# The first group's route in the fifth batch, and its rows stored in slot order as 16-bit halves and loaded turned

## The chip, the cores and the metric

One core of a Trainium2 chip. The time is the device time of one execution in microseconds (us), measured around the program; the profile's span is the part of it in which instructions are recorded. Engines: PE (TensorE) multiplies and turns, DVE (VectorE) and ACT (ScalarE) do elementwise work and read PSUM, POOL (GpSimd) does elementwise work and issues all indirect DMAs (gathers and scatters), SP (SyncE) issues the plain and the transposing DMAs. Each engine runs its instructions in program order and waits on semaphores.

## What is computed

The input x is (8, 512, 128) in fp32: 8 batches of 512 tokens of 128 features. The reference, cut to what matters (fp32; `LN` is a layer norm without gain):

```python
x = x + 0.5 * ffn(LN(x))             # fp4 quantized and dequantized in blocks of 16, inner size 352
x = x + attention(LN(x))             # 16 heads of 64, softmax over 512 keys, output projection
x = x + 0.5 * ffn(LN(x))             # the same weights again
x = x + 0.5 * moe(LN(x))             # 8 experts, the best 2 for each token, inner size 256
x = x + linear_attention(LN(x))      # 6 layers with residual, gain and bias
x = x + 0.5 * moe(LN(x))             # the same experts again
```

In `moe`, each token is gated with `x @ Wg.T`, its two best experts are taken with softmaxed weights, and each expert computes `(h1 * sigmoid(h1) * h2) @ W3.T` with `h1 = x @ W1.T`, `h2 = x @ W2.T`.

## The kernel before, in words

**Tiles.** One batch is a tile of 128 partitions x 4 chunks x 128 features. x of all 8 batches stays in SBUF (`xs`). Everything is fp32; 16-bit types serve only to move fp32 data through the transposing DMA, as two halves of each number.

**Start.** `load_x` loads the batches. The weights of the fp4 FFN are loaded into a pool of their own (`wraw`, L300 to L308), quantized (`quantize`, L425 to L470: scale on DVE, product on POOL, rounding on DVE), turned on PE (L492, L498), and that pool is closed. Then the FFN of batch 0 runs (`feed_forward`, L510): x is quantized (L446 to L467), turned (L419), multiplied by gate and up (L535), `h` is quantized in two halves, turned (L576) and multiplied by the down weights (L594); L619 adds to x.

**Attention.** `attention` (L630) goes through 64 pairs of heads, g = 0 to 63, eight a batch, about 16.8 us each. `scores` and `softmax` (L684 to L718) give `pe`; POOL copies it into halves (`pe_h`, L712), SP stores it (`pe_d`), and SP's transposing DMA brings part of it back turned (`aT`); the rest is turned on PE (L741). `widen` (L771 to L779) makes on POOL the tile `wide` from the row sums, which SP stores (`wide_d`) and loads turned as `r`; DVE needs it for `oT` (L763). `times_v` (L755) multiplies with the values, and after eight pairs `project_out` (L796) adds to x (L800). The list `ORDER` (L806) is written by hand: for each pair it says in which order PE and SP get `scores`, `transfer`, `turn`, `times_v`, `project` of this pair, the pair before and the next one. DVE, ACT and POOL follow a scheduler there.

Four slots of `ORDER` are called "ffn". In each, `beside()` (L861) takes one step of a queue of other work: the first FFN of a later batch (queued at "next", two pairs before the batch two ahead), the second FFN of a finished batch (queued when `project_out` has run), and `first_route` (L1605), the route of group 0 (batches 0 to 3), queued after the second FFN of batch 5, at g = 48. A step ends ahead of each PE operation; `Plan.pause` makes an empty step. `Route` (L954) normalizes the four tiles (`xh`), stores them in DRAM (`xg`, L970), gates them on PE (L980), picks the two best experts (`choose`, L1000), ranks the tokens in each expert by a PE product (`ranks`, L1013), gives each a place in 40 slots of 128 rows (`bases`, `places`), and from these makes the tables `tokens` (which token stands in a row; `tokens_part`, L1096: DVE and POOL make `in_slot` and `at_row` at L1103 to L1118, PE sums at L1126), `places` and `rows`. After that, `first_route` gathers the first two quads (4 slots each) of rows.

**After attention.** From here all five engines follow `Plan.order` (L115), which lists operations by planned costs in ns, with critical paths as priorities and an offset per stage from the table `LATER` (L62), which makes a stage's operations less urgent by so many ns (more urgent if negative). The stages: the second FFN of batch 7; experts of group 0 (phase 0); route and experts of group 1 (batches 4 to 7), called (0,1); the linear attention of 6 layers for two batches at a time (`linear`, L1401); then route and experts of both groups again (phase 1).

`experts` (L1213) takes 10 quads of 4 slots. For each: 4 gathers on POOL bring the rows of 4 slots (`xgs`, L1193), PE turns them (`turn4`, L419), ACT copies the turned tile (`xgT`, L1233), PE multiplies (L1245), ACT and DVE form `g` (L1250, L1254), PE turns it (L1273) and ACT copies it (`gT`, L1278), PE multiplies by W3 (L1293), ACT copies `yo` (L1302). The results go to DRAM, either scattered to the tokens' places by 4 scatters on POOL (`yt`, L1309; groups with phase equal to group) or stored in slot order by SP (`yg`). `combine` (L1338) then loads (L1347, after scatters) or gathers (L1362, after stores) two results for each token and DVE adds them (L1370). Tiles of a quad are taken from rings of 2 (xgs: two early ones and one); the next user waits for the last user of the tile.

The linear layers' weights (about 2 MB) are loaded by SP at the start of this part.

Of the kernel before, what the change touches and what calls it, by code (L numbers as in the profile page):

```python
# [17 lines left out]
P = 128  # L18
# [26 lines left out]
class Op:  # L45
# [16 lines left out]
    ("combine", 0, 1): 7000,  # L62
    ("combine", 1, 0): -31000,
    ("combine", 1, 1): 152000,
    ("experts", 0, 0): 6000,
    ("experts", 1, 0): 91000,
    ("experts", 1, 1): 33000,
    ("linear", 0): 11000,
    ("linear", 2): 7000,
    ("linear", 6): 5000,  # L70
    ("route", 1, 0): -8000,
    ("route", 1, 1): 76000,
# [3 lines left out]
class Plan:  # L76
# [38 lines left out]
    def order(self, banks):  # L115
        ops = [x for x in self.ops if x is not None]
        rank = {}
        for op in ops[::-1]:
            op.next = []
        for op in ops:  # L120
            for x in op.after:
                x.next.append(op)
        for op in ops[::-1]:
            rank[op] = op.ns + max((rank[x] for x in op.next), default=0)
        waits = {op: len(op.after) for op in ops}
        left = {op: len(op.users) for op in ops}
        ready = {e: [] for e in ("PE", "DVE", "ACT", "POOL", "SP")}
        free = dict.fromkeys(ready, 0)
        events, number, done = [], 0, []
        bank_of = {}  # L130

        def at(t, what, x):
            nonlocal number
            number += 1
            heapq.heappush(events, (t, number, what, x))

        for op in ops:
            if not waits[op]:
                at(0, "ready", op)
        banks = list(banks)  # L140
        while events:
            now = events[0][0]
            while events and events[0][0] <= now:
                _, _, what, x = heapq.heappop(events)
                number += 1
                if what == "ready":
                    heapq.heappush(ready[x.engine], (x.behind - rank[x], number, x))
                elif what == "bank":
                    banks.append(x)
            for e, heap in ready.items():  # L150
                if free[e] > now:
                    continue
                kept = []
                while heap:
                    item = heapq.heappop(heap)
                    op = item[-1]
                    if op.bank and not banks:
                        kept.append(item)
                        continue
                    if op.bank:  # L160
                        bank_of[op] = banks.pop(0)
                    done.append(op)
                    busy = max(op.ns - self.STARTS.get(e, 0), 20)
                    if e == "POOL" and op.ns > 3000:
                        busy = 1250
                    if e == "SP":
                        busy = 360
                    free[e] = now + busy
                    at(free[e], "free", None)
                    end = now + op.ns  # L170
                    for x in op.next:
                        waits[x] -= 1
                        x.start = max(getattr(x, "start", 0), end + self.SEMAPHORE)
                        if not waits[x]:
                            at(x.start, "ready", x)
                    for x in op.after:
                        if op in x.users:
                            left[x] -= 1
                            if not left[x]:
                                at(end, "bank", bank_of[x])  # L180
                    break
                for item in kept:
                    heapq.heappush(heap, item)
        assert len(done) == len(ops)
        return [(op, bank_of.get(op)) for op in done]
# [25 lines left out]
STORE = 3600  # L211


@with_exitstack
def macaron_kernel(
# [83 lines left out]
    of_weights = ExitStack()  # L299
    wpool = of_weights.enter_context(tc.tile_pool(name="wq4", bufs=1))  # L300
    wraw = wpool.tile([P, NW], F32, name="wraw")
    nc.vector.memset(wraw[:, 2 * P : 3 * P], 0.0)
    nc.vector.memset(wraw[:, 5 * P : 6 * P], 0.0)
    for i, w in enumerate((w_gate, w_up)):
        for r, (k0, kn) in enumerate(FK):
            col = (3 * i + r) * P
            nc.scalar.dma_start(wraw[:kn, col : col + P], w[k0 : k0 + kn, :])
    nc.scalar.dma_start(wraw[:, 6 * P :], w_down)  # L308
# [171 lines left out]
    with of_weights, misc_pool("w_m", 2) as misc:  # L480
        plan = Plan()
        wq4, _ = quantize(
            plan, lambda name, shape: wpool.tile(shape, F32, name=name), lambda: wraw, "w4", NW, []
# [26 lines left out]
    def feed_forward(plan, t, mem, after=None):  # L510
# [89 lines left out]
        for c in range(NC):  # L600
            for i in range(2):
                hidden(c, i)
                if c == 3 and i == 0:
                    parts.append(turn([0, 1], [0, 1], qs))
            if c % 2 == 1:
# [4 lines left out]
                qs.append(op)  # L610
        for _ in range(WAIT):
            plan.pause()
# [17 lines left out]
    def attention(first_route):  # L630
        scale = DH**-0.5
        with tc.tile_pool(name="a_sb", bufs=2) as sb, tc.tile_pool(
# [159 lines left out]
            def project_out(b):  # L792
# [19 lines left out]
                ("turn_old", 3),  # L812
                ("scores", 1),
                ("project", 1),
                ("project", 2),
                ("transfer", 0),
                ("ffn",),
# [5 lines left out]
                ("next",),  # L823
                ("ffn",),
# [12 lines left out]
            def ffn(t):  # L837
                plan = Plan()
                feed_forward(plan, t, mem)
# [7 lines left out]
            for _ in ffn(0):  # L847
# [20 lines left out]
            for g in range(NPT + 1):  # L868
                new, old, nxt = g < NPT, g > 0, g + 1 < NPT
                for what, *args in ORDER:  # L870
                    if what == "ffn":
                        beside()
                    elif what == "scores" and new:
# [22 lines left out]
                    elif what == "out" and old and g % NPAIR == 0:  # L896
                        b = g // NPAIR - 1
                        project_out(b)
                        if b < NB - 1:
                            queue.append([ffn(b), 0, -1])  # L900
                        if b == NB - 3:
                            queue.append([first_route(sb), 0, -1])
                    elif what == "next":
                        if g % NPAIR == NPAIR - 2 and g // NPAIR + 2 < NB:
# [3 lines left out]
            while queue:  # L908
                beside()
            pe_order.close()  # L910
# [20 lines left out]
            dram.tile([MG * TT, D], F32, name=f"xg{i}"),  # L931
            dram.tile([NR * P if i else 2 * MG * TT + NR * P, D], F32, name=f"yg{i}"),
# [21 lines left out]
    class Route:  # L954


        def __init__(self, plan, tiles, after, xg, mem, place, name):
# [6 lines left out]
            def tile_part(i):  # L964
# [3 lines left out]

                def store(_):
                    nc.sync.dma_start(  # L970
# [20 lines left out]
                stores.append(plan.add("SP", STORE, store, [a]))  # L991
# [92 lines left out]
            ch = plan.add("DVE", 12 * 290 + 600, choose, taken)  # L1084
            rk = plan.add("PE", product(n * E, 2), ranks, [ch], bank=True)
# [58 lines left out]

            for k in range(2 * MG):
# [51 lines left out]

    class Ring:
# [14 lines left out]
    def experts(plan, route, tiles, xg, yt, rings, spacer, number, last, scattered, early, stage):  # L1213
# [4 lines left out]
        def quad(q):  # L1218
            ks = range(q * QS, (q + 1) * QS)
            (x, x_after), (xT, xT_after) = xgs.take(), xTs.take()  # L1220
# [8 lines left out]
                for s in range(min(QS, NS - q * QS) if q >= early else 0)  # L1229
            ]  # L1230
            t = plan.add("PE", turns(QS), lambda ps: turn4(ps, x), [*got, *xT_after], bank=True)
            turned = plan.add(
                "ACT", act(TT), lambda _: nc.scalar.copy(flat(xT), t.tile), uses=[t]  # L1233
            )
            xgs.used(t)
# [365 lines left out]
    EARLY = 2  # L1601
    kept = {}
    early_xgs = [const.tile([P, QS, D], F32, name=f"xgs{q}") for q in range(EARLY)]

    def first_route(sb):  # L1605
# [9 lines left out]
        def place(what, i):  # L1615
            if what == "xh":
                return norm.tile([P, NC, D], F32, name="xh", tag="xh")
            return sb.tile([P, TT], F32, name="xqT", tag="xqT")

        plan = Plan()  # L1620
        r = Route(plan, xs[:MG], [None] * MG, scratch[0][0], mem, place, "r0")
        yield from plan.steps(banks["misc"], "misc")
        r.over()
        kept["route"] = r
        for q in range(EARLY):
            for s in range(QS):
                gather(early_xgs[q], q, s, r, scratch[0][0])
# [4 lines left out]
    with tc.tile_pool(name="post", bufs=1) as post, tc.tile_pool(  # L1632
# [3 lines left out]
        def new(name, shape, dtype=F32):  # L1636
            return post.tile(shape, dtype, name=name, tag=name)

        wqkv_sb = load(
            "wqkv_sb", [P, DEPTH, 2 * D], w_qkv[:, :, : 2 * D].rearrange("l d c -> d l c"), nc.sync, post  # L1640
        )
        wvT_sb = load("wvT_sb", [P, DEPTH, D], w_vT.rearrange("l d c -> d l c"), nc.sync, post)
        wout_sb = load("wout_sb", [P, DEPTH, D], w_out.rearrange("l d c -> d l c"), nc.sync, post)
        bout_sb = load("bout_sb", [P, DEPTH, D], b_out.partition_broadcast(P), nc.sync, post)
        weights = (wqkv_sb, wvT_sb, wout_sb, bout_sb)
        ys = [new(f"y{b}", [P, NC, D]) for b in range(NB)]
# [3 lines left out]
        def rings(name):  # L1650
            return [
                Ring(
                    (early_xgs if what == "xgs" else [])
                    + [new(f"{what}{name}{i}", shape) for i in range(n)]
                )
                for what, n, shape in (
                    ("xgs", 1, [P, QS, D]),
# [56 lines left out]
        for ph in range(2):  # L1714
            for g in range(2):
                bs = range(g * MG, (g + 1) * MG)
                tiles = [xs[b] for b in bs]
                xg, *yts = scratch[g]
# [7 lines left out]
                if ph:  # L1726
# [5 lines left out]
                    finals(g) if ph else None, g == ph, 0 if g or ph else EARLY, (ph, g),  # L1732
                )
# [18 lines left out]
        for op, bank in plan.order(range(8)):  # L1752
# [51 lines left out]
```

## Time and profile before

| | before |
|---|---|
| time, median of 3 runs | 1904.55 us (1903.48 to 1907.25) |
| the profiled execution's own time | 1905.12 us |
| its span | 1903.4 us |
| its mean PE clock | 0.943 |
| start, up to the first FFN's end for batch 0 | 0 to 58 us |
| attention, up to the last `project_out` | about 66 to 1146 us |
| experts of group 0 and 1, phase 0, PE's part | 1148 to 1346 us |
| linear attention, first PE operation after its wait | from 1394 us |
| experts, phase 1, to the end | to 1903 us |

In the profile's lines an instruction group is shown as line, engine, operation, output <- inputs, with shapes and count. "[4.11 <-DVE rsum L775]" says that the engine was idle for 4.11 us before it, and what it waited for last. In a list of waits the columns are: the waiting operation, what released it, total us, times, longest. DMA-issuing instructions of SP do not count as busy time; those of POOL (DMA_INDIRECT) appear in the timeline with the time they hold POOL.

### The profile page before, as it was taken

The page shows a single profiled execution, that of the slowest core. Times are in us where ns is not written, and L with a number is a line of the kernel's source. Part 1 is how long each engine was busy: PE and PEld are TensorE (multiplying, and loading weights), DVE is VectorE, ACT ScalarE, POOL GpSimd, SP SyncE. Part 2 cuts the span into 40 slices and gives each one's busy share as a digit, 9 for nine tenths or more (in the row PEclk, how much of TensorE's full clock was granted, in tenths as well). Part 3 has the DMA queues.
Part 4 walks back from the last instruction along what each step waited for, and adds up shares of the span by engine and source line. Part 5 has one row for each costly group of instructions (what it writes and reads, how often), then busy time and mean ns, then how long its engine had stood idle before and what let it go on. Part 6 is the DMA issues. An engine that isn't in the chain of part 4 may idle for free.

```text
span 1903.4 us, 32313 instructions
## 1 busy us (share of the span) xinstructions
PE 1679.7 (88%) x10249; PEld 1137.9 (60%) x10249; DVE 1284.4 (67%) x3266; ACT 1072.2 (56%) x2842; POOL 955.7 (50%) x1643
## 2 busy tenths in 40 slices
PE   2799999999999999999998998989659998798953
PEld 2455655656556556556665566656548887666632
DVE  4465766776776776676667657557879998666543
ACT  2466666566675675666763554445447776353521
POOL 1334454353453453443443537676664444375775
PEclk9799999999999999999998999799979999698977
DMA  5377667568666675775774772125100000022323
GB/s 167 80 171 168 144 153 183 140 151 185 154 147 149 167 172 141 166 176 134 171 183 101 177 172 78 55 46 125 44 15 1 1 1 1 23 64 61 75 75 101
DMA packets 439253, 215.10 MB, mean 113 GB/s; under 512 B 349648, under 2 KB 392848, under 8 KB 439088
## 3 DMA queue, kind: packets, MB, share of 16 engines
q1 hardware_dynamic: 428608, 192.95, 42.7%
q0 software_dynamic: 9536, 19.55, 4.5%
q8 instruction: 86, 1.41, 0.3%
q14 instruction: 79, 0.65, 0.1%
q10 hardware_dynamic: 944, 0.54, 0.1%
HBM read 28.53 MB, written 100.53 MB: 68 GB/s over the span
## 4 chain that ended last, share of the span: by engine, by line
PE 48%; DVE 24%; POOL 10%; ACT 9%; issue 5%; DMA 3%; SPq 0%; POOLq 0%; DVEq 0%; ACTq 0%
PE pS L691 8%; PE po L755 8%; ACT pe L703 4%; PE pT L741 3%; PE bank L1245 3%; DVE nmax L700 3%; PE bank L1293 2%; PE bank L535 2%; PE bank L594 2%; PE pv L677 2%; PE bank L1126 2%; PE pk L669 2%; PE bank L419 2%; POOL yt L1309 2%; PE pq L663 2%
## 5 line engine op out<-in xcount | busy, mean ns | idle before, releaser
L703 ACT ACTIVATE pe<-pS,nmax 128x512 f32<-128x512 f32 x512 | 348.4, 688 | 168.1 <-DVE nmax L700 137.0
L700 DVE TENSOR_REDUCE nmax<-pS 128x2 f32<-128x1024 f32 x256 | 310.6, 1214 | 75.0 <-PE pS L691 74.5
L712 POOL COPY pe_h<-pe 128x1024 uint16<-128x1024 uint16 x256 | 272.7, 1092 | 153.0 <-ACT pe L703 74.2
L691 PE MATMUL pS<-kT,qT 64*128 64x512 f32 x1024 | 291.9, 647 | 0.2
L755 PE MATMUL po<-aT,v 128*64 128x256 f32 x2048 | 237.6, 383 | 3.0 <-DMA aT<-pe_d 2.1
L779 POOL COPY wide<-rsum 128x512 uint16<-128x512 uint16 x128 | 76.5, 627 | 290.7 <-DVE rsum L775 290.7
L755 PEld LDWEIGHTS po<-aT,v 128*64 128x64 f32 x2048 | 142.2, 137 | 118.3 <-ACT pe L703 23.5
L1245 PE MATMUL bank<-wall,xgT 128*128 x320 | 150.9, 609 | 6.7 <-ACT xgT L1233 4.9
L741 PE MATMUL pT<-ident,pe 128*128 128x128 f32 x1024 | 137.3, 276 | 4.8 <-ACT pe L703 4.6
L741 PEld LDWEIGHTS pT<-ident,pe 128*128 128x128 f32 x1024 | 116.9, 141 | 23.0 <-ACT pe L703 17.8
L744 ACT COPY aT<-pT 128x512 f32<-128x512 f32 x192 | 107.5, 599 | 22.6 <-PE pT L741 21.0
L1254 DVE SCALAR_TENSOR_TENSOR g<-g,bank 128x256 f32<-128x256 f32 x160 | 66.7, 417 | 74.5 <-ACT g L1250 74.2
L691 PEld LDWEIGHTS pS<-kT,qT 64*128 64x128 f32 x1024 | 77.7, 186 | 57.7 <-issue 44.9
L556 DVE SCALAR_TENSOR_TENSOR h<-h,bank 128x176 f32<-128x176 f32 x120 | 39.5, 329 | 105.1 <-ACT h L553 105.1
L535 PEld LDWEIGHTS bank<-wgu,xqT 128*128 128x128 f32 x480 | 77.4, 197 | 47.0 <-issue 18.9
L419 PE MATMUL bank<-ident,work 128*128 128x128 f32 x436 | 72.4, 293 | 35.9 <-DVE work L402 25.1
L703 ACT ACTIVATION_READ_ACCUMULATOR pe<-pS,nmax 128x1 f32 x512 | 103.6, 202 | 0.0
L535 PE MATMUL bank<-wgu,xqT 128*128 128x176 f32 x480 | 97.5, 329 | 6.3 <-ACT xqT L531 4.3
L1250 ACT ACTIVATE g<-bank 128x256 f32<-128x256 f32 x160 | 60.0, 386 | 67.0 <-PE bank L1245 52.9
L1245 PEld LDWEIGHTS bank<-wall,xgT 128*128 128x128 f32 x320 | 56.7, 193 | 66.1 <-issue 31.7
L763 DVE TENSOR_TENSOR oT<-po,r 128x256 f32<-128x256 f32 x128 | 51.9, 419 | 65.5 <-DMA r<-wide_d 43.2
L1498 ACT ACTIVATE work<-bank,nmk 128x128 f32<-128x128 f32 x192 | 68.1, 370 | 45.8 <-DVE nmk L1490 44.8
(400 smaller groups left out, 3675.4 us busy)
## 6 DMA issues: line engine op xcount, KB each, us to landing
pe_d<-pe_h SPq DMA_DIRECT2D x256, 256.0 KB, 2.4
wide_d<-wide SPq DMA_DIRECT2D x64, 256.0 KB, 2.0
aT<-pe_d SPq DMA_TRANSPOSE x256, 3.9
xg<-work SPq DMA_DIRECT2D x12, 256.0 KB, 2.6
yg<-yo SPq DMA_DIRECT2D x10, 256.0 KB, 3.3
yt<-yo SPq DMA_DIRECT2D x10, 256.0 KB, 2.3
x<-in_x SPq DMA_DIRECT2D x8, 256.0 KB, 4.6
yk<-yg SPq DMA_DIRECT2D x8, 256.0 KB, 4.2
```

Of the source, the lines that this page charges most:

```text
L419: nc.tensor.transpose(ps[:, c, :], src[:, c, :], ident)
L535: nc.tensor.matmul(ps[:, j * FH : (j + 1) * FH], m["xqT"][:, c * P : (c + 1) * P], wgu[:, j, cols], start=True, stop=True,)
L691: nc.tensor.matmul(ps[:, j, :], qTs[g][rows, c * P : (c + 1) * P], kTs[g][rows, :], start=True, stop=True,)
L700: nc.vector.tensor_reduce(nmax, ps, AX.X, ALU.max, negate=True)
L703: nc.scalar.activation(pe[:, j, :], ps[:, j, :], AF.Exp, bias=nmax[:, j : j + 1], accum_out=sums[g][:, 2 * c + j : 2 * c + j + 1],)
L712: nc.gpsimd.tensor_copy(split, pe[:, j, :].bitcast(U16).rearrange("p (n h) -> p h n", h=2))
L741: nc.tensor.transpose(ps[:, k, :], pe[:, j, k * P : (k + 1) * P], ident)
L744: nc.scalar.copy(dst, ps)
L755: nc.tensor.matmul(po[rows, :], vs[g][:, k, rows], aT[:, :, j, k, :], start=(k == 0), stop=(k == NC - 1),)
L779: nc.gpsimd.tensor_copy(split[:, h, :].rearrange("p (n d) -> p n d", d=DH), src[:, h, :, None].to_broadcast([P, NC * 2, DH]),)
L1245: nc.tensor.matmul(ps, xT[:, s, :], wall[:, bass.ds(at[s], 2 * HID)], start=True, stop=True)
L1498: nc.scalar.activation(c4(ek)[:, c, :], pk.tile[:, c * D : (c + 1) * D], AF.Exp, bias=nmk[:, i, c : c + 1], accum_out=sk[:, i, c : c + 1],)
```

## The change

1. **Start.** The fp4 weights are loaded into the memory of the attention's `oT` tile, within `attention`. The FFN of batch 0 takes its first three steps, then the weights are quantized, then it goes on. For this one FFN (`alone`) the first turns of `h` come after all 16 gate and up products instead of before the last pair.
2. **The queue.** The first FFN of batch 7 is queued at g = 40 and `first_route` right behind it, when batch 4's output is projected (before: g = 46 and g = 48). In `Route`, three pauses come after `choose` and two before the token parts.
3. **Halves.** For group 0 in phase 0 POOL copies `xh` into 16-bit halves (`divide`, four copies of 128x1024, in the ring of `pe_h`) and SP stores these.
4. **Sorting.** Once the route is done, each pair has three "sort" slots: in each POOL gathers one slot's 128 rows of halves (64 KB, ring of 6 tiles), and SP stores the slot gathered before in slot order. After 40 slots quad 0 is loaded turned. What is not done by the last pair is done behind it.
5. **Experts of group 0, phase 0.** SP loads each quad turned by one transposing DMA (128x1024 of 16 bits, `xgT`); the gathers, PE's turns and ACT's copies of these ten quads are gone. The ring of `xgs` gets two tiles of its own.
6. **Linear weights.** They are loaded when 80 operations of the plan are out, instead of at the beginning.
7. **`LATER`.** Offsets change: combine(1,0) from -31000 to 109200, route(0,1) new at -105500, route(0,0) new at 28300, experts(1,1) 33000 to 53300, combine(1,1) 152000 to 138200, the others by less than 1000.

In the program order that follows, the experts of phase 1 look so on POOL: before, one scatter, 32 gathers of combine(1,0), 38 scatters; after, the scatters with runs of 1, 2, 4 and 2 combine gathers between them, and the last 24 gathers behind them. The final stores of batches 4 to 7 come ahead of those of 0 to 3.

```diff
 LATER = {
-    ("combine", 1, 0): -31000,
-    ("combine", 1, 1): 152000,
-    ("experts", 1, 1): 33000,
+    ("combine", 1, 0): 109200,
+    ("combine", 1, 1): 138200,
+    ("experts", 1, 1): 53300,
+    ("route", 0, 0): 28300,
+    ("route", 0, 1): -105500,
...
-                if c == 3 and i == 0:
+                if c == 3 and i == 0 and not alone:
                     parts.append(turn([0, 1], [0, 1], qs))
...
+        if alone:
+            parts.append(turn([0, 1], [0, 1], qs[:1]))
...
                 ("turn_old", 3),
+                ("sort",),
                 ("scores", 1),
                 ("project", 1),
                 ("project", 2),
                 ("transfer", 0),
+                ("sort",),
                 ("ffn",),
...
                 ("next",),
+                ("sort",),
                 ("ffn",),
...
-            for _ in ffn(0):
+            wraw = weights_mem("wraw", [P, NW])
+            load_weights(wraw)
+            first = ffn(0)
+            for _ in range(3):
+                next(first)
+            quantize_weights(wraw, weights_mem, misc)
+            for _ in first:
                 pass
...
+                        if b == NB - 4:
+                            queue.append([ffn(NB - 1), 0, NB - 1])
+                            queue.append([first_route(sb), 0, -1])
                         if b < NB - 1:
                             queue.append([ffn(b), 0, -1])
-                        if b == NB - 3:
-                            queue.append([first_route(sb), 0, -1])
...
+                def divide(_):
+                    r["xh_h", i] = place("xh_h", i)
+                    nc.gpsimd.tensor_copy(
+                        r["xh_h", i].rearrange("p (c h d) -> p c h d", h=2, d=D),
+                        r["xh", i].bitcast(U16).rearrange("p c (d h) -> p c h d", h=2),
+                    )
...
             ch = plan.add("DVE", 12 * 290 + 600, choose, taken)
+            for _ in range(3):
+                plan.pause()
...
+            for _ in range(2):
+                plan.pause()
             for k in range(2 * MG):
                 tokens_part(k)
...
+    def load_turned(xT, there):
+        nc.sync.dma_start(
+            flat(xT).bitcast(U16), there.rearrange("s p h d -> (s p h) d"), transpose=True
+        )
...
+                if q >= early:
+                    turned = plan.add(
+                        "SP", LOAD_TURNED, lambda _: load_turned(xT, in_order[q]), [*xT_after]
+                    )
...
+    def sorting(sb):
+        r = kept["route"]
...
+        for k in range(NR):
+            x = sb.tile([P, 2 * D], U16, name="rows", tag="rows", bufs=6)
+            nc.gpsimd.indirect_dma_start(
+                x, None, scratch[0][1][:, :],
+                bass.IndirectOffsetOnAxis(ap=r.tokens[:, k : k + 1], axis=0),
+            )
+            if stores:
+                nc.sync.dma_start(*stores.pop())
+            stores.append((there[k // QS][k % QS].rearrange("p h d -> p (h d)"), x))
+            yield 1
...
+            if i == 80:
+                load_linear()
```

## The prediction

> **What bounds the kernel now.** I read the shares of the page first, then the windows by stage, then PE's waits in the stages with idle time, and at last single stretches of the timeline.
>
> ```profile
> PE 1679.7 (88%) x10249; PEld 1137.9 (60%) x10249; DVE 1284.4 (67%) x3266; ACT 1072.2 (56%) x2842; POOL 955.7 (50%) x1643
> ...
> PE   2799999999999999999998998989659998798953
> ...
> PEclk9799999999999999999998999799979999698977
> ```
>
> PE is busy 88% of the span, so what can be won is what PE idles (224 us) and what is taken off it. The row of slices puts the idle time at the very start, in the slices after attention (which ends at 1146), near 1370 and at the end.
>
> The windows (length, then busy time of PE, PEld, DVE, ACT, POOL, then PE's clock, the DMA share and GB/s):
>
> ```profile
> 0.00:50.00 50.00, 12.25 (x49) 10.40 (x49) 24.60 (x67) 11.32 (x23) 8.47 (x26) 0.89 0.52 159
> 700.00:850.00 150.00, 146.98 (x934) 90.06 (x936) 105.62 (x212) 100.34 (x253) 70.51 (x116) 1.00 0.71 166
> 1000.00:1146.00 146.00, 133.83 (x876) 86.34 (x872) 94.03 (x207) 73.16 (x183) 60.64 (x76) 0.96 0.63 146
> 1146.00:1250.00 104.00, 94.49 (x482) 69.68 (x483) 70.67 (x228) 46.04 (x105) 72.42 (x117) 0.89 0.23 64
> 1250.00:1346.00 96.00, 86.65 (x430) 57.66 (x430) 66.50 (x216) 48.24 (x107) 67.67 (x124) 0.95 0.34 83
> ```
>
> Steady attention is PE at 98%; its last stretch is PE at 92%; the two stretches after it leave PE idle for 9.5 and 9.4 us. The waits of PE name the largest single holes: of 1000 to 1146, then of 1346 to 1400, then of 1760 to 1904:
>
> ```profile
> PE bank L1126 <- POOL in_slot L1118: 9.6, 3, 8.3
> ```
> ```profile
> PE bank L419 <- DVE work L402: 24.9, 1, 24.9
> ```
> ```profile
> PE bank L1273 <- ACT yo L1302: 21.2, 1, 21.2
> ```
>
> The first is the route of group 0: its token tables are asked of PE while DVE and POOL are still making them. The second stands before the linear layers: DVE's norm waits for combine gathers on POOL. The third is in the last experts: the ring of `yo` is full, since its scatters stand on POOL behind 32 combine gathers (1797.6 to 1836.4).
>
> **The change part by part**, against the profiled execution (1905.12 us, span 1903.4), which is 0.6 above the median of 1904.55.
>
> *Start.* The first FFN begins before the weights are quantized, and its first h transposes go behind all 16 gate and up matmuls.
>
> ```profile
> 28.30 6.55 PE L535 MATMUL bank<-wgu,xqT 128*128 128x176 f32 x28 [0.68 <-ACT xqT L531]
> 41.84 1.12 PE L576 MATMUL bank<-ident,h_mg 128*128 128x128 f32 x4 [6.99 <-POOL h_mg L467]
> 42.75 1.38 PE L535 MATMUL bank<-wgu,xqT 128*128 128x176 f32 x4
> 52.01 1.97 PE L576 MATMUL bank<-ident,h_mg 128*128 128x128 f32 x8 [7.88 <-POOL h_mg L467]
> ```
>
> Now x's quantization starts on DVE at 21.02 after 4.72 us idle for the weights' transposes; with xh ready at 15.12 and DVE free at 16.30 it could start 4.7 earlier, which moves L535 from 28.3 to 23.6. The last pair (42.75) no longer stands behind the 6.99 us wait, so the second quantization of h (45.26 to 51.95, 6.7 us) follows the first at 35.7 and ends near 42.4. The gain is 51.95 - 42.4 = 9.5 us, between 7 (if the weights' transposes come later than now) and 11. Nothing overlaps it: PE has only this to do.
>
> *The route moved by eight pairs, with pauses.* Three empty steps stand between `choose` and the ranks and two before the token parts, so POOL's `in_slot` has time: the waits of 9.6 us go (8.3 to 9.6). Route work itself only moves within attention.
>
> *Sorting beside attention.* Before, 8 gathers went out in one burst and held up `wide` until 1075.43:
>
> ```profile
> 1074.48 0.95 POOL L1193 DMA_INDIRECT xgs<-xg,tokens  x1 [0.30 <-issue]
> 1075.43 1.16 POOL L779 COPY wide<-rsum 128x512 uint16<-128x512 uint16 x2
> ```
>
> aT then came at 1081.7, for 1.1 us of PE's time (0 to 2): gone. Instead 40 gathers of 64 KB go out, three a pair over some 14 pairs, on POOL between the last `pe_h` of a pair and the next `wide`; each is followed by a store on SP one batch later, when its gather has landed. A gather holds POOL 0.95 + 0.30 = 1.25 us, so 3.75 a pair. The gap they go into:
>
> ```profile
> 961.35 1.17 POOL L779 COPY wide<-rsum 128x512 uint16<-128x512 uint16 x2 [4.11 <-DVE rsum L775]
> ```
>
> 4.1 to 4.6 us, in some pairs with 1.38 of `h_mg` in it. So a pair with `h_mg` makes `wide` some 0.5 to 1 us late, and DVE's oT already waits for r in 5 of 36 places of 700 to 1000 (7.6 us), while PE stays at 98%. I take 4 us in all (0.3 a pair), between 0 and 15 (1.1 a pair). The stores put 40 issues of 0.34 to 0.57 on SP beside 20 transfers a pair; they move 2 x 2.6 MB in 235 us, 22 GB/s beside 166. With the four `divide` copies (1.04 each, in the ring of `pe_h`, which `pe_d` stores then release later) and this traffic I put 2 us (0 to 6). The six turned issues of quad 0 and later quads are 1.3 each on SP.
>
> *After attention.* Removed: 32 gathers (40 us of POOL, which is busy 72 of 104), 10 turns of a quad on PE (0.60 each, 0.44 net of overlap, so 4.4) and 10 ACT copies. Added: 9 turned loads on SP. As a row for them stands aT (the same 256 KB by the same DMA kind): 3.9 us to land, 1.3 to issue. A quad takes PE 8 to 8.8 us, and two tiles are in turn, so they are covered from the second on; the first of them can only go out when attention's memory is free (1146), and is hidden by quad 0, loaded before. If that cover is gone the price is 4 to 5 us once. The linear weights (2 MB) move behind the loads; they are needed near 1370. POOL's freed time lets scatters leave at once, and the second FFN of batch 7 and route(0,1) come earlier: I read the tokens of group 1 some 10 us earlier than 1248. Of the 18.9 us that PE idles in 1146 to 1346, half stays with turns inside a quad (waits for g and gT). So 4.4 + 9 = 13 (3 to 17). The 24.9 us hole stays: combine(0,1)'s gathers remain one run behind the last scatter.
>
> The Trainium skill speaks against the turned load: "VectorE: DVE Perf Modes", section "The three transpose paths", has 128x128 of 16 bits at 390 ns on TensorE and 1309 ns by DMA, and advises TensorE where PSUM will do. An estimate from that page: eight blocks a quad are 10.5 us, over a quad's 8.8, which would add 1.7 x 9 = 15 us and put the whole near 1884. The trace's 3.9 us for the same size speaks against that.
>
> *Tail.* The combine of group 0 is spread over the last scatters (runs of 2 and 4, and 24 at the end) instead of 32 ahead of 38 scatters; group 1's outputs come first. POOL's indirect work in 1668 to 1886 is 149 x 1.26 = 188 of 218 us, so POOL paces the tail. Before, 17.6 us follow the last POOL operation (loads of 5.5, 8 adds, stores); after, a gather's landing 2.6, one add 1.14 and a store of 3.6, about 7. That is 10 us less if POOL never idles for PE, and I take 8 (3 to 12), since the 21.2 us hole of PE need not become time. The new LATER values of experts(1,1) and combine(1,1) make this order; the others change by at most 0.6 us of planned time beside the two routes and combine(1,0), and I count them at nothing.
>
> **Sum.** -9.5 - 9.6 - 1.1 + 4 + 2 - 13 - 8 = -35.2: 1905.1 becomes 1869.9 for the profiled run and 1869.3 for the median; I say 1869.
>
> **The rivals.**
> A, forecast: 0.54, at 1858 to 1881.
> B, the stages after attention hardly shorten: the chain FFN(7), route(0,1), tokens bounds them (POOL's gathers were hidden; PE busy 94.5 of 104 speaks for it, POOL at 70% against) and the tail stays with PE. Then mid is -3 and tail -3: 1869 + 10 + 5 = 1884, in 1881 to 1892. 0.22.
> C, slower: on POOL the three gathers delay `wide` in each of 14 pairs; SP's r, and the aT behind it, then arrive late and PE waits. Price up to 3.75 x 14 = 52.5 in place of 4: 1869 + 48.5 = 1917. It decides from 39.2/14 = 2.8 us a pair. For it is oT's waiting on r, against it the gap of 4.1 us. With such a delay in part, 1892 to 1917. 0.10.
> D, the turned load does not come in time at the start of post: +4.5, 1874, within A.
> E, better: the hole of 24.9 shrinks by some 8, as combine gathers start earlier, and POOL is gapless in the tail: 1869 - 8 - 2 = 1859, with the other good ends down to 1852. 0.14.
>
> The ends of the terms, taken as independent, add up to +16 and -7; with B on one side and E on the other the range is 1853 to 1889. About 0.2% (3.8 us) is what a measurement of this kernel can tell from no change, so same is 1900.7 to 1908.4. Of C's 0.10, some 0.01 falls below that, 0.02 in it and 0.07 above: faster 0.91, same 0.02, slower 0.07.
>
> **What would show it.** After: L594's first matmuls near 44.5, not 53.8; no wait of PE on in_slot; `wide` waits of POOL with gathers before it, oT's wait on r about as now; attention ending near 1129 to 1135; no turn of `xgs` with `tokens`, first L1245 just after that; the tokens_B gathers near 1225; the (0,1) experts ending 28 or so earlier than 1346; no 21 us hole on `yo`; and a gather as POOL's last. Wrong if PE waits for aT or xgT more than 10 us in all, if attention ends after 1146, or if PE's holes reappear in the tail behind POOL's scatters.

## The result, and the profile after

The changed kernel takes 1925.69 us (median; 1924.89 to 1927.52) beside 1905.36 for the kernel before: the ratio is 1.0112, 95% interval [1.0098, 1.0126]. The prediction was 1869, in 1853 to 1889; it was wrong, and on the wrong side. The profiled execution took 1924.89 us with a span of 1922.9.

The page's busy line and its rows of slices:

```profile
PE 1682.4 (87%) x10209; PEld 1135.7 (59%) x10209; DVE 1284.2 (67%) x3266; ACT 1068.9 (56%) x2832; POOL 961.4 (50%) x1648
...
PE   3799999999999999999999988978848999699980
...
PEclk8899999999999999999999998979979999789995
```

There are 40 matmuls fewer, and PE is busy longer: 1682.4 against 1679.7 us. The row of slices hides the loss: a 9 stands for 90% and more, so attention shows nines nearly up to its end, as it did before, though from 850 to 1000 PE fell from 147.5 to 141.9 us of 150. Only times of events show where it is.

Four times divide the span (last x addition of attention, on DVE; first PE operation of the linear layers; end):

| | before | after | difference | predicted |
|---|---|---|---|---|
| attention's end | 1145.8 | 1176.8 | +31.0 | -14.2 |
| from there to the linear layers | 248.4 | 242.8 | -5.6 | -13 |
| from there to the end | 509.3 | 503.3 | -6.0 | -8 |

So the parts after attention went the way that was forecast, together at about half the size. Attention is wrong by 45 us; its end after 1146 is one of the prediction's own signs of being wrong. Its windows, from the first pair to the last x addition, for the kernel before and the changed one (columns as in the prediction):

```profile
70.00:1145.80 1075.80, 1039.43 (x6527) 641.59 (x6525) 724.09 (x1446) 684.80 (x1726) 474.33 (x722) 0.99 0.69 159
```
```profile
62.00:1176.80 1114.80, 1057.60 (x6527) 651.81 (x6525) 725.49 (x1449) 685.28 (x1726) 504.89 (x758) 0.98 0.68 158
```

The same 6527 matmuls: PE's idle time grows from 36.4 to 57.2 us, and its busy time from 1039.4 to 1057.6. Nearly half of the loss is not waiting but slower matmuls; the last section traces them to the granted clock. PE's waits from 640 to 1000 and from 1000 to 1177 name what was late:

```profile
PE pT L748 <- ACT pe L710: 7.0, 5, 2.5
PE bank L1175 <- POOL in_slot L1167: 3.6, 3, 2.4
```
```profile
PE bank L581 <- DVE oT L770: 10.8, 3, 4.0
PE py L803 <- DVE oT L770: 3.0, 1, 3.0
```

The wait on `in_slot` fell from 9.6 to 3.6; the forecast had it gone. New is `oT`: DVE waits for `r`, which SP loads after POOL has made `wide`. POOL, SP and DVE in one pair (start, length, the idle time before in brackets):

```profile
1116.92 0.97 POOL L1700 DMA_INDIRECT rows<-xh,tokens  x1 [2.44 <-DMA xs<-rows]
1122.62 0.94 POOL L1700 DMA_INDIRECT rows<-xh,tokens  x1 [4.72 <-DMA xs<-rows]
1124.63 1.03 POOL L1700 DMA_INDIRECT rows<-xh,tokens  x1 [1.07 <-DMA xs<-rows]
1125.67 1.16 POOL L786 COPY wide<-rsum 128x512 uint16<-128x512 uint16 x2
```
```profile
1118.36 0.57 SPq L1705 DMA_DIRECT2D xs<-rows  x1
1118.97 2.59 SPq L774 DMA_TRANSPOSE aT<-pe_d  x2
1121.66 0.53 SPq L1705 DMA_DIRECT2D xs<-rows  x1
```
```profile
1120.85 0.14 DVE L782 RECIPROCAL rsum<-rsum 128x8 f32<-128x8 f32 x1
...
1132.54 0.76 DVE L770 TENSOR_TENSOR oT<-po,r 128x256 f32<-128x256 f32 x2 [2.81 <-DMA r<-wide_d]
```

The row sums are ready at 1121.0, and `wide` starts at 1125.7. Ahead of it on POOL stand three gathers, and the last two wait for stores that SP issues at 1118.4 and 1121.7, between transposing loads of 1.3 us each. The ring has 6 tiles, six gathers go out at the start in one burst, and from then on each gather needs the tile of the gather six before it: the one whose store is being issued just now.

### The profile page after: what moved, and what is told of

It reads as the page before. It is cut to its first block, busy times and chain, and to the rows that moved or that the text cites. A ratio compares the mean times of both kernels' runs of the same rounds, so it can differ in the third digit from the quotient of the medians.

```text
span 1922.9 us, 32375 instructions
## 1 busy us (share of the span) xinstructions
PE 1682.4 (87%) x10209; PEld 1135.7 (59%) x10209; DVE 1284.2 (67%) x3266; ACT 1068.9 (56%) x2832; POOL 961.4 (50%) x1648
## 4 chain that ended last, share of the span: by engine, by line
PE 47%; DVE 25%; ACT 10%; POOL 10%; issue 5%; DMA 3%; SPq 1%; POOLq 0%; DVEq 0%; ACTq 0%
PE pS L698 7%; PE po L762 7%; PE bank L1308 4%; ACT pe L710 4%; DVE nmax L707 4%; PE pT L748 3%; PE bank L1356 3%; PE bank L599 2%; PE bank L540 2%; PE bank L423 2%; PE py L803 2%; PE bank L1175 2%; PE pv L684 2%; POOL work L1425 2%; PE pk L676 2%
## 5 line engine op out<-in xcount | busy, mean ns | idle before, releaser
L719 POOL COPY pe_h<-pe 128x1024 uint16<-128x1024 uint16 x256 | 268.0, 1073 | 139.3 <-ACT pe L710 70.6
L698 PE MATMUL pS<-kT,qT 64*128 64x512 f32 x1024 | 296.3, 656 | 2.5 <-ACT pe L710 2.3
L684 PEld LDWEIGHTS pv<-wv_sb,hT 128*128 128x128 f32 x512 | 66.4, 193 | 41.7 <-ACT aT L751 18.6
```

What stands on the lines that cost most here:

```text
L684: nc.tensor.matmul(ps[:, c, :], hT[:, c * P : (c + 1) * P], wv_sb[:, cols(g)], start=True, stop=True,)
L698: nc.tensor.matmul(ps[:, j, :], qTs[g][rows, c * P : (c + 1) * P], kTs[g][rows, :], start=True, stop=True,)
L719: nc.gpsimd.tensor_copy(split, pe[:, j, :].bitcast(U16).rearrange("p (n h) -> p h n", h=2))
```

## The experiments

Four theories: (1) gathers that wait for stores hold up `wide`; (2) the gathers' own POOL time and traffic cost, wherever they stand; (3) the new start upsets the order of the engines in all of attention; (4) the moved queue entries cost, by the norm of batch 7's FFN or by themselves. Times of whole kernels stand beside those of the kernel before: 1904.5 for e1 to e4, 1904.3 for e5 to e8, 2011.6 for e9 to e11, 2017.1 for e12 and e13. These four groups ran on four chips. On the last two, the stages after attention took some 90 to 140 us longer in every kernel (why is open), so of those five runs mainly attention is read. "Attention's end" is the last x addition, and a pair is dated by SP's issue of its `wide_d`, in one trace of each run. Up to pair 35 all fourteen kernels with the new start do the same work, and this pair comes 5.2 to 7.3 us before that of the kernel before, on all chips: a difference of under some 2 us between two ends says nothing.

**e1_start.** The first FFN ahead of the weights alone, on the kernel before.

```diff
-            for _ in ffn(0):
+            wraw = weights_mem("wraw", [P, NW])
+            load_weights(wraw)
+            first = ffn(0)
+            for _ in range(3):
+                next(first)
+            quantize_weights(wraw, weights_mem, misc)
+            for _ in first:
...
```

> The kernel before with the new start alone (FFN of batch 0 begins ahead of the weights' quantization, its first h turns behind all 16 products). In the changed kernel the first pairs run 8.4 us earlier, 6.4 by pair 35, and then 8 to 10 us are lost in pairs 36 to 40, ahead of any sort. Theory 1 (the loss belongs to the sort and the moved route): here the start's gain holds to the end, 8 us less, about 1897. Theory 3 (the start shifts how DVE, ACT and POOL are ordered all through attention, and that costs in pairs 36 to 40): the gain is gone there, about 1905.

1896.95 us, ratio 0.9963 [0.9951, 0.9976]. The first pair is 7.7 us earlier and attention ends at 1139.1, 6.7 earlier. Theory 3 falls: in pairs 36 to 40 the lead is still 7.0.

**e2_no_sort_beside.** The changed kernel with the sort behind the last pair.

```diff
-                ("sort",),
...
-            for _ in kept["sorting"]:
+            for _ in sorting(sb):
```

> The changed kernel without the sort slots in the pairs: all 40 gathers and stores come behind the last pair. Theory 1 (gathers stand ahead of the tile wide on POOL and wait there for stores on SP): attention ends near 1137 to 1142 instead of 1176.8, and the sort costs some 50 us of POOL after it, so that the whole is near 1925 again. Theory 2 (POOL time and traffic of the gathers themselves, wherever they stand): the same here. Theory 3 (order of DVE and ACT in other pairs): attention still ends above 1160 and the whole is above 1940.

1950.88 us. Attention ends at 1152.7, 24 us earlier than in the changed kernel, and then PE waits 48.4 us for the first turned load. So the sort costs 24 us where it is; but without it attention still ends 13.6 us later than in e1. Something else costs too, and none of the three theories had both numbers right.

**e3_gathers_pinned.** Each gather in program order on POOL.

```diff
-            nc.gpsimd.indirect_dma_start(
+            op = nc.gpsimd.indirect_dma_start(
...
+            tc.keep_in_program_order(op)
```

> The changed kernel with each gather kept in program order on POOL, so that a gather comes at its own slot, two pairs after the store that frees its tile. Number of gathers and stores, bytes and SP's order are as in the changed kernel. Theory 1: no gather waits for a store, wide comes in time, attention ends near 1150, the whole near 1898. Theory 2: no difference beyond 5 us, about 1920 or more.

1909.15 us, 16.5 less than the changed kernel, and attention ends at 1158.7. The gathers' groups, from 940 to the end of attention, in the changed kernel and in e3 (busy, mean ns | idle before, with what ended it):

```profile
L1700 POOL DMA_INDIRECT rows<-xh,tokens x40 | 39.6, 989 | 96.8 <-DMA xs<-rows 86.3 <-DVE h_rs L455 7.1 <-issue 2.6
```
```profile
L1700 POOL DMA_INDIRECT rows<-xh,tokens x40 | 39.5, 987 | 15.4 <-issue 7.1 <-DMA xs<-rows 6.0 <-DVE tok L1212 0.8
```

The same 40 gathers, of the same length: 86.3 us of waiting for stores became 6.0. This is theory 1, and 18.1 us of attention; the end near 1150 that it had forecast did not come.

**e4_gathers_behind_wide.** Each gather behind the last `wide`.

```diff
+            with tc.issue_after(kept["wide"]):
+                nc.gpsimd.indirect_dma_start(
```

> The changed kernel with each gather ordered behind the last wide traced before it: three gathers right behind wide instead of ahead of it. Theory 1: wide is never behind a gather that waits; attention ends near 1148, the whole near 1897; the gathers now delay the copies pe_h by up to 3.75 us a pair, which may give some back. Theory 2: 1918 or more.

1924.02 us, attention's end 1174.6. The expectation failed, although the waits are gone here as well:

```profile
L1701 POOL DMA_INDIRECT rows<-xh,tokens x40 | 40.9, 1023 | 16.1 <-DMA xs<-rows 5.9 <-issue 4.3 <-ACT pe L710 2.1
```

Three gathers in a row right behind `wide` hold POOL for 3.7 us where it next has the copies `pe_h`, which SP and the aT loads wait for: from 940 on SP waits 63.1 us for `pe_h`, against 42.0 in e3. So theory 2 is right at this place: POOL time alone can cost as much. In e3 the gathers lie one between two pairs of copies and two behind them, and cost nothing that can be seen against e5 below.

**e5_start_queue.** The new start, the moved queue entries and the pauses; no sort, no halves, the old `LATER`.

```diff
+                        if b == NB - 4:
+                            queue.append([ffn(NB - 1), 0, NB - 1])
+                            queue.append([first_route(sb), 0, -1])
...
+            for _ in range(3):
+                plan.pause()
```

> The new start, plus the moved queue entries (first FFN of batch 7 and the route at g = 40) and the pauses; no halves, no sort, no turned loads, the old LATER. The kernel with the new start alone ends its attention at 1139. Theory 4 (moving the FFN of batch 7 lets its norm run in pair 36 beside two others and costs some 8 us there; the route's move costs some 5 more in pairs 44 to 51; the stall of 9.6 us on in_slot goes): attention ends near 1145 to 1150, the whole near 1904 to 1908. Theory 1 (only the sort costs): attention ends near 1130, the whole near 1888.

1917.88 us, attention's end 1159.4, 20.3 later than e1 and 0.7 later than e3. This is the largest single loss, about twice what theory 4 had expected, and the sort has no part in it.

**e6_start_pauses.** The new start and the pauses alone.

```diff
+            for _ in range(3):
+                plan.pause()
...
+            for _ in range(2):
+                plan.pause()
```

> The new start, plus the pauses of 3 and 2 steps in the route, everything else as before (route after g = 48, old gathers). If the stall of 9.6 us on in_slot comes from the tables being asked for too early, it is gone here and the whole is near 1888 to 1890 against 1897 with the start alone. If DVE and POOL have no time for the tables beside attention wherever they stand, the wait only moves, and it stays near 1897.

1900.13 us against 1896.95 for e1: the wait on `in_slot` falls from 9.6 to 1.8 us, and nothing is won. Pair 57 comes 10.1 us earlier than in e1, pair 63 only 0.6, and attention ends 3.5 later (1.5 of this stand there at pair 35). From pair 56 to attention's end PE idles 10.4 us, against 11.0 in e1, for the same 806 matmuls: the wait only moved. The five empty steps make the queue longer than the pairs, so the last FFN's second half runs with nothing beside it, behind a late softmax:

```profile
1124.22 1.97 PE L742 MATMUL pT<-ident,pe 128*128 128x128 f32 x8 [4.30 <-ACT pe L704]
```

**e7_start_later.** The new start and the new `LATER` table.

```diff
-    ("combine", 1, 0): -31000,
+    ("combine", 1, 0): 109200,
...
```

> The new start, plus the new LATER table alone (old attention, old experts). In the changed kernel the time from the end of the linear layers' part to the end fell by some 5 us, and PE's wait of 21 us on yo is gone. If that is the table's doing: 1897 less 5, near 1892. If it needs the turned loads or the other ring: within 2 us of 1897.

1894.48 us, ratio 0.9951 [0.9939, 0.9964]: 2.5 less than e1, half of what was expected (the two intervals overlap; from attention's end on the traces have 753.3 us against 755.8). PE's wait of 21 us on `yo` is gone. It is the fastest kernel measured here, faster than both.

**e8_pinned_and_norm.** e3, and the norm and x quantization of batch 7's FFN in program order.

```diff
-                return plan.steps(misc, "misc")
+                return plan.steps(misc, "misc", tc if pinned else None)
```

> The kernel with the gathers in program order, and in it the first steps (norm and quantization of x) of the FFN of batch 7 also kept in program order on DVE, POOL and ACT, so that they come at g = 40 and not in pair 36 beside two other norms. Theory 4: the loss of 8 us in pairs 36 to 40 goes, attention ends near 1151, the whole near 1901 against 1909. Rival (the loss in these pairs has another cause): within 2 us of 1909.

1906.88 us, attention's end 1156.0: nearer the rival than theory 4. In pair 36 of the changed kernel three norms run at once on DVE and POOL, and softmax stands behind them:

```profile
664.33 0.17 DVE L350 TENSOR_TENSOR t_m<-t_st 128x4 f32<-128x4 f32 x1 [2.37 <-POOL t_s L373]
...
668.58 1.22 DVE L707 TENSOR_REDUCE nmax<-pS 128x2 f32<-128x1024 f32 x1
```
```profile
666.34 1.13 PE L698 MATMUL pS<-kT,qT 64*128 64x512 f32 x4
...
670.73 1.33 PE L748 MATMUL pT<-ident,pe 128*128 128x128 f32 x8 [2.47 <-ACT pe L710]
...
672.76 2.08 PE L698 MATMUL pS<-kT,qT 64*128 64x512 f32 x4
```

With the norm in order e8 is 9.4 us ahead of e3 at pair 39 (1.4 at pair 35), and 2.7 at the end of attention. The norm now stands in pair 41; pairs 41 and 42 alone lose 5.2, and in e12, which has the same order, ACT waits there 4.35 us for POOL's part of the norm, ahead of `pe`.

**e9_start_queue_no_pauses.** e5 without the pauses.

> The new start and the moved queue entries without the pauses; all else as before. With the pauses the whole was 1917.9 and attention ended 20 us after that of the new start alone. Theory 4a (the five empty steps push the last FFN of the queue behind the last pair, some 4 us, and the rest is the moved work itself): the spill goes, but the stall on in_slot of some 8 to 10 us comes back at its new place; the whole between 1915 and 1925. Theory 4b (the pauses are what costs): near 1900.

Attention's end 1150.9, 11.9 later than e1 and 8.4 earlier than e5 (ratio of the whole 1.0048 [1.0030, 1.0066]). The stall on `in_slot` is back, in pair 49, with 11.8 us:

```profile
PE bank L1140 <- POOL in_slot L1132: 13.1, 3, 11.8
```

So the pauses cost 8.4 with the moved queue (1.8 of this stand there at pair 35), and the moved work 11.9: 4a is right in kind, its spill twice the size.

**e10_stores_first.** The changed kernel, its three sort slots at the first place of the pair.

```diff
                 ("turn_old", 3),
                 ("sort",),
+                ("sort",),
+                ("sort",),
...
-                ("sort",),
...
-                ("sort",),
```

> The changed kernel with its three sort slots of a pair one after the other at the first place, so that SP issues the three stores ahead of the pair's later pe_d stores and the aT transposes; the gathers keep their ring of 6 tiles and their free order on POOL, still ahead of wide. Theory 1 (gathers wait there for stores that SP issues late, and wide with them): the stores land some 5 us earlier, the waits shrink; attention ends 8 to 16 us earlier than 1176.8, the whole between 1910 and 1918. Theory 2 (order and number of gathers ahead of wide cost by themselves, 3.75 us a pair): within 4 us of 1925.7.

Attention's end 1161.8, 15.0 earlier than in the changed kernel (ratio of the whole 0.9967 [0.9955, 0.9979]). The stores come earlier in SP's order, the gathers stand ahead of `wide` as before; their waits on stores fall from 86.3 to 23.6 us:

```profile
L1700 POOL DMA_INDIRECT rows<-xh,tokens x40 | 39.2, 981 | 33.3 <-DMA xs<-rows 23.6 <-issue 8.0 <-DVE tok L1212 0.8
```

Theory 1 again, from the other end of the wait.

**e11_start_later_two_pauses.** e7 and the two pauses ahead of the token parts.

```diff
+            for _ in range(2):
+                plan.pause()
```

> The new start, the new LATER table, and two pauses ahead of the token parts alone (the stall of 8.3 us is at the first of them; half a pair is 8.4 us). It leaves three steps fewer to spill behind the last pair than all five pauses. If the stall can be had without the spill: near 1888 to 1891. If any pause is given back at the end of attention: 1894 to 1898, as with five.

Attention's end 1144.7, 5.2 later than e7's 1139.5. Pair 57 is 6.9 us earlier than in e7, pair 63 is 3.8 later: in attention the pauses are given back, as with five. (Ratio of the whole 1.0099 [1.0062, 1.0137]; from attention's end on the trace has 890.1 us, beside 863.8 in e9 on the same chip, for a reason that is open.)

**e12_queue_norm_pinned.** e9 with the norm in order.

> The new start and the moved queue entries without pauses, and the norm and x quantization of the FFN of batch 7 kept in program order. Without that order attention ended 11.9 us after that of the new start alone (1150.9 against 1139.1), 8 to 10 of it by pair 40. Theory 4 (the early norm in pair 36 is what moving the queue costs; the stall on in_slot only changes its place): attention ends near 1141 to 1144. Rival (the moved work costs wherever its norm stands, and what is won in pair 36 is lost in the pairs behind, as with the pauses): 1148 or later.

Attention's end 1150.2 against 1150.9: pair 40 is 9.2 us earlier than in e9, pair 51 only 1.0. The rival holds (whole: ratio 1.0008 [0.9992, 1.0025]).

**e13_all_repairs.** e8 without the pauses.

> The changed kernel without the pauses, with its gathers and the norm of batch 7 in program order. With gathers in order and pauses it took 1909.2, attention ending at 1158.7. Theory 1 and 4 together (gathers that wait cost 18, pauses 8, the early norm 8 to 10 of the loss): attention ends near 1142 to 1146 and the whole is 12 to 16 us under the run with ordered gathers, near 1894 to 1897 where the kernel before takes 1904.5. Rival (PE at 98% gives back whatever a repair wins): above 1904.

Attention's end 1165.2, later than e8's 1156.0. The repairs do not add up; the expectation failed. The ratio of the whole, 0.9943 [0.9924, 0.9961], fits it by luck alone: from attention's end on e13 takes 840.7 us, against 864.3 in e12 on the same chip, and this hides the later end. Here the stall of 11.8 is back, and PE waits once 5.7 us for aT.

**What attention's 31 us are made of**, by the ends of attention: the start -6.7 (e1), the moved queue +11.9 (e9), the pauses +8.4 (e5), halves and sort with ordered gathers -0.7 (e3; less than two traces can tell), the gathers' free order +18.1. The steps add up to the total because each starts from the one before; e13 shows that in another order they would come out differently. Within the 11.9, PE's idle time in pairs 36 to 45 (some 7.6 us more than e1) and a longer stall (12.5 in its pair against 8.9) are seen; why the moved work finds less room there was not settled.

## Why the prediction was wrong, point by point

*Start: right.* Foretold 9.5 (7 to 11), measured 7.5 for the whole (e1). In the changed kernel the gate and up products start at 24.84, not 23.6, and the down product at 46.35 instead of 53.77; near 44.5 was foretold.

*The stall: the step that fails in principle.* The wait fell to 3.6 us (1.8 in e6), and nothing of its 9.6 us was won. I took a wait of PE for a loss that is won when it is removed, and did not ask what the empty steps push back: they move the queue's end behind the last pair, and the pairs behind the former stall became longer. e6, e11, and e5 beside e9 show it three times. That DVE, ACT and POOL had used the stall to catch up would explain the longer pairs; no run shows this by itself.

*"Route work itself only moves within attention": the step of the largest error.* It was counted at nothing, and costs 11.9 alone and 20.3 with the pauses. Moving queue entries also lets the scheduler pull their first instructions forward, as batch 7's norm into pair 36; but keeping that norm in order won 0.7 at the end (e12), so it alone is not the cause.

*The sort: right place, wrong reason and size.* +4 with bounds of 0 and 15; measured 18 in the changed kernel. I priced the gathers' 3.75 us in a gap of 4.1 and saw that each store finds its gather landed. I did not follow the ring the other way round: that a gather needs its tile's store, and that SP issues that store behind the transposes. Rival C named the right path (`wide`, r, oT, PE) with a price of POOL time alone; it decided with less than its 2.8 us a pair (18.1 / 14 = 1.3) because the other gains did not come. It was given 0.10, with an end of 1917, and the time lies beyond that. The +2 for halves and traffic cannot be told from nothing: with ordered gathers halves and sort together measured -0.7. (SP has 10 transfers a pair, not 20, and ten turned loads, not six; no term hangs on these counts.)

*After attention: in part rival B.* -5.6 instead of -13. The first gather of group 1's rows stands 104.0 us behind attention's end before, and 101.6 after:

```profile
1249.76 0.94 POOL L1193 DMA_INDIRECT xgs<-xg,tokens_B  x1 [0.30 <-DMA xgs<-xg,tokens]
```
```profile
1278.36 1.01 POOL L1244 DMA_INDIRECT xgs<-xg,tokens_B  x1 [4.96 <-DVE tokens_B L1208]
```

POOL was freed of 32 gathers and is busy for 48.2 of the 104.0 us behind attention's end, where it was 72.2; what it then waits for is the tables of the chain FFN(7), route(0,1). B's price for this part was -3, and its other half, a tail of -3, did not come. The hole ahead of the linear layers stayed, at 23.8 us, as foretold. The turned loads were never waited for: they landed in 3.2 us (median of 9). So the 1309 ns for each 128x128 in the Trainium skill ("VectorE: DVE Perf Modes", "The three transpose paths"), from which the prediction estimated 10.5 us a quad, is no measure for this transfer.

*Tail: right, a term short.* -6.0 from the linear layers on instead of -8. The hole on `yo` went, and POOL ran to the last gather (the 32 combine gathers stand there as runs of 2, 4, 2 and 24). But one gather took 6.26 us instead of 0.95, while DVE ran the adds of combine(1,0) and (1,1) without a break from 1889.6 to 1897.8:

```profile
1891.14 0.96 POOL L1425 DMA_INDIRECT work<-yt,rows_A  x1 [0.30 <-issue]
1892.40 6.26 POOL L1425 DMA_INDIRECT work<-yt,rows_A  x1 [0.30 <-issue]
```
```profile
1889.89 3.23 DVE L1433 SCALAR_TENSOR_TENSOR x<-work,m_B,x 128x128 f32<-128x128 f32 x12
...
1897.24 0.60 DVE L1433 SCALAR_TENSOR_TENSOR x<-work,m_A,x 128x128 f32<-128x128 f32 x2
```

The gather ends at 1898.66, 0.82 us behind the last of these adds. The eight loads of combine(1,1), issued 11 to 5 us before, give DVE so many adds at once; in the kernel before they stand behind POOL's last operation. e2, e3, e4, e8, e10 and e13 have one such gather of 6.0 to 6.8 us, e7 and e11 two shorter ones, of 2.1 to 3.6; the last section shows that all end alike. The prediction had no term for it.

Slower matmuls made the error larger: in attention e1 has 35.5 us of idle PE and 1041.5 of busy, the changed kernel 57.2 and 1057.6 for the same matmuls. With 21.7 us of waits more, 16.1 us of slower matmuls came on top.

## What to carry to other kernels

Follow a ring of buffers in both directions: the engine that fills a tile also waits for whoever empties it, and an in-order engine that waits there holds up all that stands behind it; a scheduler that fills gaps with "ready" work can run such a ring full for good. Where one engine is at 98%, a removed wait is a gain only if the queue's end does not move back by as much: look at the last pairs, not at the place of the wait. Do the parts of a large change one by one: here the start and the stage offsets alone gave 1894.5, while the sort beside attention, and the earlier route that it needs, cost more than its loads gave.

## What the runs showed of the hardware

A short wait of PE can cost more than its length. In pair 36 a wait of 2.47 us was followed by four score products in 2.08 us instead of 1.13 (the fences of e8), and the granted clock fell from 1.00 to 0.50 (the column behind the five engines):

```profile
661.00:672.30 11.30, 8.82 (x59) 5.20 (x60) 7.19 (x16) 6.77 (x18) 8.31 (x35) 1.00 0.72 153
672.30:682.60 10.30, 8.71 (x25) 4.55 (x23) 9.31 (x18) 7.60 (x20) 3.55 (x9) 0.50 0.22 57
```

Attention's slower matmuls are nearly all of this kind. While the trace has the clock at 0.5, PE was busy for 48.7 us of the changed kernel's attention, 18.9 in e1, 31.0 in e5 and 16.1 in e9; with half of that taken off, its busy time in attention is 1033.3, 1032.0, 1034.7 and 1033.7, nearly the same. So 16.1 us of slower matmuls came with 21.7 us of added waiting in the changed kernel, 8.8 with 11.6 in e5, and only 0.2 with 11.7 in e9, which has one stall of 11.8 in place of one of 8.3. The price of a wait is not fixed either: behind the same wait in pair 36 (2.47 to 2.49 us) the clock stayed at 0.5 for 10.2 us in the changed kernel, for 3.4 in e2, e4, e5, e9 and e10, and in e3 it fell only behind a second wait, of 2.74. The Trainium skill ("TensorE: Matmul & The Clock Gate", Part 1) puts the idle window that halves the clock at some 3.4 us; here waits shorter than that were enough.

A long run of adds on DVE can hold an indirect DMA on POOL. Of the 4477 indirect DMAs in the fifteen traces 13 took more than 2 us (2.1 to 6.8), and the others at most 1.64. Each of the 13 began within a run of back-to-back combine adds on DVE of 4.0 to 8.2 us, as the third or fourth indirect DMA that overlaps it, and each ended 0.82 to 0.84 us behind the last add of the run. It need not be a gather, or have loads before it: in e9 and e12 it is a scatter, here that of e9 and its run of adds, and in the 3 us before it the DMA engines were busy for a share of 0.06.

```profile
1951.05 3.63 POOL L1323 DMA_INDIRECT yt<-yo,places_B  x1 [0.19 <-issue]
```
```profile
1948.50 5.33 DVE L1384 SCALAR_TENSOR_TENSOR x<-work,m_A,x 128x128 f32<-128x128 f32 x20
```

No run changes these adds alone; that the end follows theirs in all 13 is what ties the two together.
